# A gated recurrence on one core: the four loads of wx issued from two queues in turn, the biases after them

## The chip, the cores and the metric

The kernel runs on one core of a Trainium2 chip. The metric is the time of one execution on the device in microseconds (us); of several runs the median is taken. The profile comes from one further execution.

## What is computed

Eight sequences (B = 8) of 512 steps with 512 features go through a recurrent cell with a state of 512, and its output is added to the input. All is fp32.

```python
def step(h, x_t):
    fused = sigmoid(concatenate([x_t, h], axis=-1) @ w_W + w_b)
    hidden_state, output_state = split(fused, 2, axis=-1)
    memory_state = x_t @ wx_W + wx_b + hidden_state * (h @ wh_W + wh_b)
    h_new = output_state * h + (1.0 - output_state) * tanh(memory_state)
    return h_new, h_new

_, hs = scan(step, h0, swapaxes(x, 0, 1))    # 512 steps, h0 = cond_1024
return x + swapaxes(hs, 0, 1)
```

The 512 steps depend on each other; only the products of x with its weights can be made ahead.

## The kernel before

The 512 features lie as 4 quarters (k) of 128 partitions. The weights are held in SBUF in three tiles, each cut by k:

- `wx`: the weights that multiply x, four parts of 768 KB (128 rows of 6 KB each), loaded at L118 to L120;
- `wgr`: the weights of the state for the banks R and G, four parts of 512 KB (L122 to L124);
- `whh`: those for bank H, one load of 768 KB for three parts and one of 256 KB for the fourth (L125 to L127).

Three smaller things are loaded too. `head` (L92, L93; 144 KB) holds x of the first eight steps and the initial state. `rows4` (L114 to L116; 8 KB) is set to zero, and the four rows of biases go into four of its partitions. x itself comes in chunks of 16 steps: `load_x` (L96) loads the second half of chunk 0 at L132, chunks 1 to 3 after the first three steps (L374), and later ones as buffers come free.

A load is issued by an engine's queue. Here SyncE's queue issues everything but `head` and the biases, which ScalarE's queue issues before ScalarE's first arithmetic, the loading of its function table and a sigmoid of one column (L158). A load signals through one of eight completion counters, handed out in the order of the program; the ninth load takes the first counter again and its issue waits until the load that had it has landed.

The work that precedes the recurrence stands in the kernel in this order, and each engine does its part of it in this order:

1. TensorE starts its banks with zeros (L184) and multiplies zeros twice (L189, `warm` at L190), each as two records of 512 columns.
2. The bias matmul (L191) spreads `rows4` over the partitions by a matrix `ones`, into the PSUM bank `xp0`. It needs the biases landed.
3. VectorE copies that bank to the tile `bias` (L193) and the initial state into its tiles (L196). ScalarE's `seed` (L213) copies `bias` into the other bank, `xp1`.
4. `prefill(0)` (L215) adds, into `xp0`, the products of x of the first four steps with `wx`: for each k four matmuls of 384 columns side by side, two records each, so 8 records for a quarter and 32 in all. The quarter k needs part k of `wx`. It begins after VectorE's copy, since it adds to what the copy reads.
5. One more `warm`; ScalarE's `spread` (L230) copies `xp0` into the banks R, G and H; VectorE's `turn_x` (L235) transposes a part of it.
6. Step 0 (FIRST, L29): TensorE does the state's products for R and G, quarter by quarter ("Q0" to "Q3", from `wgr`), with the four quarters of `prefill(1)` between them ("x"), and then bank H (from `whh`). From step 1 on the order is that of L27, with one quarter of the next group's prefill behind it.

In every step VectorE transposes the banks and ScalarE takes sigmoids and a tanh of them; VectorE's scan (L283) makes the new state, in two halves, `hTA` and `hTB`, and TensorE's next matmuls on bank R need `hTA`. Of matmuls all records stand at L178 (the helper `mm`), so they are told apart by their tiles.

The loads touched by the change are these, with the helper for x between them and `head`:

```python
nc.scalar.dma_start(out=head, in_=xh)                     # L93
...
nc.vector.memset(rows4, 0.0)                              # L115
nc.scalar.dma_start(out=rows4[0:128:32], in_=bias_d)      # L116
...
for k in range(NQ):
    nc.sync.dma_start(out=wx[:, k], in_=wx_d[k])          # L120
```

Of the kernel before, what the change touches and what calls it, by code (L numbers as in the profile page):

```python
# [36 lines left out]
def tile_cond_rnn_residual(  # L37
# [39 lines left out]
    nc = tc.nc  # L77
# [35 lines left out]

    rows4 = const.tile([P, 512], F32, name="rows4")  # L114
    nc.vector.memset(rows4, 0.0)  # L115
    nc.scalar.dma_start(out=rows4[0:128:32], in_=bias_d)  # L116

    wx = const.tile([P, NQ, NQ, 384], F32, name="wx")  # L118
    for k in range(NQ):
        nc.sync.dma_start(out=wx[:, k], in_=wx_d[k])  # L120

    wgr = const.tile([P, NQ, NQ, 256], F32, name="wgr")  # L122
    for k in range(NQ):
# [134 lines left out]
    for i in range(T):  # L258
# [8 lines left out]
        for n in (ORDER if i else FIRST).split():  # L267
# [3 lines left out]
            bank, k = n[0], int(n[1])  # L271
# [210 lines left out]
```

## Time and profile before

| | |
|---|---|
| median of 3 runs | 1693.86 us (1693.85 to 1693.97) |
| the profiled execution | 1693.49 us |
| its span, first to last instruction | 1691.7 us |
| granted TensorE clock over the span | 1.000 |
| PE busy | 1680.3 us, 99% of the span |
| DVE, ACT, POOL busy | 64%, 54%, 14% of the span |
| DMA | 30.86 MB in all; mean 18 GB/s over the span |
| DMA in 3 to 7 us, 7 to 11, 11 to 15, 15 to 18 | 410, 423, 420, 411 GB/s |
| SyncE's issues of wx | 4 from 0.74 us, 0.38 to 1.05 us each |
| wx, issue to landing | 5.1 to 9.3 us, median 7.2 |
| ScalarE's issue of head | 0.74 us, lasting 0.42; 5.2 to landing |
| ScalarE's issue of the biases | 1.43 us, lasting 1.09 |

PE is TensorE's matmul, PEld its loading of weights, DVE VectorE, ACT ScalarE, POOL GpSimd, SP SyncE; SPq and ACTq are the queues by which an engine issues loads. A row of the timeline has the start, the length, the engine, the line of the kernel, the operation, the tile written and the tiles read, the shape and the number of instructions merged; in brackets stands how long the engine had been idle before, and what ended that by the profile. Releasers are inferred from the events of semaphores, so where several things were awaited the name can be wrong. Matmuls overlap, so a record is longer than the time from one start to the next. In a table by stages the columns are the stage, its length, busy time and count of instructions of PE, PEld, DVE, ACT and POOL, the granted clock, the share of the 16 DMA engines that was busy, and GB/s.

### The profile page before, as it was taken

The page shows a single profiled execution, that of the slowest core. Times are in us where ns is not written, and L with a number is a line of the kernel's source. Part 1 is how long each engine was busy: PE and PEld are TensorE (multiplying, and loading weights), DVE is VectorE, ACT ScalarE, POOL GpSimd, SP SyncE. Part 2 cuts the span into 40 slices and gives each one's busy share as a digit, 9 for nine tenths or more (in the row PEclk, how much of TensorE's full clock was granted, in tenths as well). Part 3 has the DMA queues.
Part 4 walks back from the last instruction along what each step waited for, and adds up shares of the span by engine and source line. Part 5 has one row for each costly group of instructions (what it writes and reads, how often), then busy time and mean ns, then how long its engine had stood idle before and what let it go on. Part 6 is the DMA issues. An engine that isn't in the chain of part 4 may idle for free.

```text
span 1691.7 us, 121258 instructions
## 1 busy us (share of the span) xinstructions
PE 1680.3 (99%) x53230; PEld 1467.6 (87%) x53230; DVE 1087.0 (64%) x8229; ACT 915.5 (54%) x5121; POOL 231.2 (14%) x1032
## 2 busy tenths in 40 slices
PE   8999999999999999999999999999999999999998
PEld 6888888888888888888888888888888888888887
DVE  5666666666666666666666666666666666666666
ACT  3555555555555555555555555555555555555554
POOL 0111111111111111111111111111111111111111
PEclk9999999999999999999999999999999999999999
DMA  4000000000000000000000000000000000000000
GB/s 177 17 17 5 17 17 17 17 4 17 17 17 17 4 17 17 17 17 13 9 18 17 17 17 4 17 17 17 17 5 17 17 17 17 4 17 11 11 11 10
DMA packets 11483, 30.86 MB, mean 18 GB/s; under 512 B 1220, under 2 KB 1732, under 8 KB 10952
## 3 DMA queue, kind: packets, MB, share of 16 engines
q1 hardware_dynamic: 10800, 22.94, 3.9%
q8 instruction: 416, 6.82, 1.7%
q14 instruction: 115, 0.94, 0.2%
q10 hardware_dynamic: 152, 0.16, 0.0%
HBM read 14.70 MB, written 8.39 MB: 14 GB/s over the span
## 4 chain that ended last, share of the span: by engine, by line
PE 98%; DMA 1%; DVE 0%; ACT 0%; issue 0%; SPq 0%
PE R L178 26%; PE G L178 26%; PE H L178 26%; PE xp L178 19%; DMA whh<-in_whh_dram 1%; DMA head<-in_xh_dram 0%; DVE md1A L321 0%; DVE hTA L283 0%; ACT hd0A L205 0%; ACT hTA L205 0%; SPq L124 0%; DVE tz L303 0%; ACT hTB L205 0%; DVE hTB L283 0%; ACT hd0B L205 0%
## 5 line engine op out<-in xcount | busy, mean ns | idle before, releaser
L178 PE MATMUL xp<-wx,xin 128*32 128x384 f32 x4032 | 431.3, 486 | 0.0
L178 PEld LDWEIGHTS R<-wgr,hTA 128*32 128x32 f32 x8176 | 247.4, 135 | 206.8 <-DVE hTA L283 206.4
L303 DVE STREAM_TRANSPOSE tr<-R 128x64 f32<-128x64 f32 x1022 | 194.4, 229 | 309.1 <-PE R L178 309.1
L178 PE MATMUL R<-wgr,hTA 128*32 128x128 f32 x8176 | 330.9, 273 | 2.2 <-DVE hTA L283 2.2
L178 PE MATMUL H<-whh,hTA 128*32 128x128 f32 x8192 | 331.3, 273 | 0.8 <-DMA whh<-in_whh_dram 0.8
L178 PE MATMUL H<-whh,hTB 128*32 128x128 f32 x8192 | 331.2, 273 | 0.0
L178 PE MATMUL R<-wgr,hTB 128*32 128x128 f32 x8176 | 330.6, 273 | 0.0
L178 PE MATMUL G<-wgr,hTB 128*32 128x128 f32 x8176 | 330.6, 273 | 0.0
L178 PE MATMUL G<-wgr,hTA 128*32 128x128 f32 x8176 | 330.6, 273 | 0.0
L385 POOL TENSOR_TENSOR ot<-xin,hTB 128x16 f32<-128x16 f32 x503 | 126.4, 251 | 1415.6 <-DVE hTB L283 1324.0
L205 ACT ACTIVATE hd0B<-tz 128x16 f32<-128x16 f32 x512 | 114.9, 224 | 305.3 <-DVE tz L303 305.3
L205 ACT ACTIVATE md0A<-tr 128x16 f32<-128x16 f32 x512 | 119.6, 234 | 265.2 <-DVE tr L303 265.2
L178 PEld LDWEIGHTS H<-whh,hTA 128*32 128x32 f32 x8192 | 260.2, 136 | 1.2 <-DMA whh<-in_whh_dram 1.2
L178 PEld LDWEIGHTS G<-wgr,hTA 128*32 128x32 f32 x8176 | 259.8, 136 | 0.0
L178 PEld LDWEIGHTS H<-whh,hTB 128*32 128x32 f32 x8192 | 254.5, 122 | 0.0
L178 PEld LDWEIGHTS G<-wgr,hTB 128*32 128x32 f32 x8176 | 254.1, 122 | 0.0
L178 PEld LDWEIGHTS R<-wgr,hTB 128*32 128x32 f32 x8176 | 245.2, 122 | 0.0
L283 DVE TENSOR_TENSOR_SCAN hTA<-hd0A,hTA 128x48 f32<-128x48 f32 x512 | 132.1, 258 | 149.2 <-ACT hTA L205 149.2
L283 DVE TENSOR_TENSOR_SCAN hTB<-hd0B,hTB 128x24 f32<-128x24 f32 x1024 | 158.1, 196 | 104.0 <-ACT hTB L205 104.0
L205 ACT ACTIVATE hd0A<-tz 128x16 f32<-128x16 f32 x512 | 118.9, 232 | 111.4 <-DVE tz L303 111.4
L321 DVE STREAM_TRANSPOSE md1A<-G 128x64 f32<-128x64 f32 x511 | 156.8, 307 | 28.7
L205 ACT ACTIVATE hTB<-hTB 128x16 f32<-128x16 f32 x512 | 121.2, 237 | 81.1 <-DVE hTB L283 80.5
(62 smaller groups left out, 1680.2 us busy)
## 6 DMA issues: line engine op xcount, KB each, us to landing
xin<-in_x_dram SPq DMA_DIRECT2D x31, 256.0 KB, 3.8
out_dram<-ot SPq DMA_DIRECT2D x31, 256.0 KB, 3.3
wx<-in_wx_dram SPq DMA_DIRECT2D x4, 768.0 KB, 7.2
wgr<-in_wgr_dram SPq DMA_DIRECT2D x4, 512.0 KB, 9.7
whh<-in_whh_dram SPq DMA_DIRECT2D x1, 768.0 KB
whh<-in_wh_dram SPq DMA_DIRECT2D x1, 256.0 KB, 11.2
out_dram<-ot SPq DMA_DIRECT2D x1, 192.0 KB, 1.9
head<-in_xh_dram ACTq DMA_DIRECT2D x1, 144.0 KB, 5.2
```

Of the source, the lines that this page charges most:

```text
L178: nc.tensor.matmul(out_, lhsT, rhs, start=start, stop=False, skip_group_check=True)
L205: inst = nc.scalar.activation(out_, in_, func, **kw).ins
L283: nc.vector.tensor_tensor_scan(*[t_[:, :, c_].rearrange("p n c s -> p (n c s)") for t_ in (out_, d0, d1)], 0.0, ALU.mult, ALU.add,)
L303: inst = nc.vector.transpose(t_.rearrange("p c n -> p (c n)"), raw[n][hf]).ins
L321: nc.vector.transpose(md1[hf][g % 2][:, :, :, 0].rearrange("p n c -> p c n"), raw["h"][hf])
L385: return engine.tensor_tensor(ot[:, t, 2 * hf : 2 * hf + 2, :].rearrange("p c n -> p n c"), x_of(c, slice(2 * hf, 2 * hf + 2), t, 1).rearr ...
```

## The change

The loads of parts 1 and 3 of `wx` are issued by ScalarE's queue, those of parts 0 and 2 by SyncE's as before, and the load of the biases is issued by ScalarE's queue after them. In the built program SyncE's queue begins with wx 0, wx 2 and the loads of `wgr`, and ScalarE's with head, wx 1, wx 3 and the biases, ahead of the function table; the completion counters follow the new order. The instructions of TensorE, VectorE and GpSimd and their order are the same.

```diff
     rows4 = const.tile([P, 512], F32, name="rows4")
     nc.vector.memset(rows4, 0.0)
-    nc.scalar.dma_start(out=rows4[0:128:32], in_=bias_d)
 
     wx = const.tile([P, NQ, NQ, 384], F32, name="wx")
     for k in range(NQ):
-        nc.sync.dma_start(out=wx[:, k], in_=wx_d[k])
+        (nc.scalar if k % 2 else nc.sync).dma_start(out=wx[:, k], in_=wx_d[k])
+    nc.scalar.dma_start(out=rows4[0:128:32], in_=bias_d)
```

## The prediction, made before the changed kernel ran

> **What bounds the kernel now.** I read the chain that ended last first. It is PE nearly all the way, so anything that delays the first step of the recurrence by some us, with nothing later that waits and could absorb it, is added to the end. The same chain in order of time shows where PE is not yet the bound: the first 18.2 us.
>
> ```profile
> PE 98%; DMA 1%; DVE 0%; ACT 0%; issue 0%; SPq 0%
> ```
> ```profile
> 0.74 5.23 DMA head<-in_xh_dram
> ...
> 6.83 11.38 DMA whh<-in_whh_dram
> 18.21 0.04 issue
> 18.25 1.11 PE H L178 x32
> 19.36 0.65 PE xp L178 x8
> 20.01 0.44 PE R L178 x16
> ```
>
> (Columns: start, length, what.) The last wait for data is whh. Then I read the timeline of the start-up, because the change moves two loads there, and one of them, the biases, opens everything.
>
> ```profile
> 6.77 1.10 PE L178 MATMUL xp<-rows,ones 128*128 128x512 f32 x2 [0.57 <-DVE hTB L160]
> ...
> 7.91 0.69 DVE L193 COPY bias<-xp 128x512 f32<-128x512 f32 x1 [1.26 <-PE xp L178]
> ...
> 8.65 2.14 PE L178 MATMUL xp<-wx,head 128*32 128x384 f32 x24 [0.78 <-DVE bias L193]
> ...
> 11.44 0.85 PE L178 MATMUL xp<-wx,head 128*32 128x384 f32 x8 [0.64 <-DMA wx<-in_wx_dram]
> ...
> 12.36 0.25 ACT L230 COPY R<-xp 128x128 f32<-128x128 f32 x1 [3.14 <-PE xp L178]
> ...
> 13.22 0.27 DVE L235 STREAM_TRANSPOSE md1B<-xp 128x32 f32<-128x32 f32 x2
> ...
> 13.59 0.67 PE L178 MATMUL xp<-wgr,hTA 128*32 128x256 f32 x8 [0.24 <-issue]
> ...
> 18.25 0.67 PE L178 MATMUL H<-whh,hTA 128*32 128x128 f32 x16 [0.77 <-DMA whh<-in_whh_dram]
> ...
> 18.82 0.26 DVE L283 TENSOR_TENSOR_SCAN hTA<-hd0A,hTA 128x48 f32<-128x48 f32 x1 [0.36 <-ACT hTA L205]
> ...
> 19.82 0.62 PE L178 MATMUL R<-wgr,hTA 128*32 128x128 f32 x16
> ```
>
> The reader is to see a serial chain: biases landed, bias matmul (L191), VectorE's copy (L193), prefill(0) from 8.65, its last quarter held to 11.44 by the fourth part of wx, then the spreads, the transposes of L235, and step 0 at 13.59. The releaser named at 6.77 is inferred. The built program lets that matmul wait for the biases' counter and for the memsets of ones, and the latter ended at 2.21 + 0.47 = 2.68; so the biases landed at about 6.7.
>
> Last, the DMA queues (q1 is SyncE's, q10 ScalarE's: packets, MB, share), in 3.5 to 4.5 us, and then the GB/s by stages.
>
> ```profile
> q1 hardware_dynamic: 59, 0.36, 86.3%
> q10 hardware_dynamic: 58, 0.07, 18.5%
> ```
> ```profile
> 7.00:11.00 4.00, 3.01 (x26) 0.72 (x25) 1.01 (x5) 0.59 (x1) 0.00 (x0) 1.00 1.01 423
> 11.00:15.00 4.00, 3.32 (x34) 1.49 (x38) 0.51 (x4) 0.59 (x3) 0.00 (x0) 1.00 1.03 420
> ```
>
> The engines are full (share 1.01 to 1.03, 420 GB/s), so a second queue cannot bring more bytes there. While both queues hold work they are served packet for packet, 59 to 58, though a packet of wx is 6 KB and one of head 1.2 KB.
>
> **The change, part by part.** *SyncE's queue* loses two issues of about 0.4 us. Its two loads of wgr come earlier on its ring, but the ring was already fed six loads ahead of the data, so this gains nothing. The eight completion counters are handed out in program order, so the later issues wait for: wgr 2 head, wgr 3 wx 0, whh wx 1, whh3 wx 2, then the x loads wx 3, wgr 0, the biases and wgr 1. wx 1 will land at about 9.6 instead of 7.6, so whh is issued some 3 us later, with 2.1 MB of wgr still in front of it (5 us at 420 GB/s): no hole, whh lands near 18.2 as before. The x loads that now wait longer are first read from step 8 on, beyond 40 us.
>
> *ScalarE's queue* gets two issues ahead of the biases, and behind them the table load and the sigmoid of L158. An issue took 0.42 to 1.10 us in the rows, so the last of these ends near 6 instead of 4.05; ScalarE's next work waits for the bias copy (8.63 before, later now). Cost nothing.
>
> *The biases* now stand behind head, wx 1 and wx 3 on ScalarE's ring, and that ring gets every second packet. A load of 128 rows puts 8 packets and one for its counter on each of 16 engines. The biases' row is ScalarE's packet 28 (3 x 9 + 1). SyncE's ring had 26 packets done over 16 engines (1.6 each) when ScalarE's first came at 2.75 us, so by then it has served about 30: wx 0, wx 2, wgr 0 (27) and three rows of wgr 1. In MB: ScalarE 0.147 + 2 x 0.786 + 0.008 = 1.73; SyncE 2 x 0.786 + 0.524 + 3/8 x 0.524 = 2.29; together 4.02. Before, wx 3 landed at 11.4 with 3.30 MB behind it (issued at 2.1, 9.3 to landing). So the biases land at 11.4 + (4.02 - 3.30) / 0.42 = 13.1. The same reckoning for the biases of before (1.24 MB) gives 6.5 against 6.7 seen, so I take 13.2: **6.5 us later**. Bounds: shared by bytes instead of packets (2 x 1.73 + the lead 0.16 = 3.62 MB) 12.2; all of wgr 1 ahead of them (4.35 MB) 13.9.
>
> A page puts the bounds otherwise: the Trainium skill ("DMA: Bandwidth & Descriptors", section "Queues, rings and completion order") says that an engine stays on a ring for a packet of typically 9 to 17 descriptors before it switches. By that a whole load would go at a turn, and the biases would come behind wgr 1, at 13.9. The rows' even count in each quarter us (15 to 15) speaks for single rows; I keep 13.2.
>
> *What absorbs some of it.* (1) The prefill's wait for wx 3. The four quarters of prefill(0) run at 0.65 each (0.325 for four matmuls in the rows from 8.65), so the last could have begun at 8.65 + 1.95 = 10.60 and began at 11.44: 0.84 of the delay goes there, since all of wx has landed by 12.9. (2) The wait for whh at 18.25. Without it, step 1's matmuls R could begin 0.77 earlier by PE, but they also need hTA, ready at 18.82 + 0.26 = 19.08, plus the 0.15 that the next step takes from there (22.94 to 23.09): 19.23 in place of 19.82, so 0.59. Sum: 6.5 - 0.84 - 0.59 = **5.07 us**. What is late next is only PE's chain itself, all of it shifted; each further step repeats at 3.27 us.
>
> *TensorE's clock.* PE has nothing between the end of the zero matmuls (6.21) and 13.2: 7 us. Before, its longest pause after the start was under 1 us. The rows show two speeds of the same 512-column fp32 matmul, while the granted clock reads 1.00 in both:
>
> ```profile
> L178 PE MATMUL xp<-zeros 128*128 128x512 f32 x4 | 3.5, 1036 | 0.0
> ```
> ```profile
> L178 PE MATMUL xp<-rows,ones x2: 592/630/667, 6.8 to 7.3; 128*128 128x512 f32 x2
> ```
>
> At 2.69, 3.64 and 4.49 one started each 0.85 us; at 6.77 the pair ran at 0.51. So a PE that had been idle ran slow from 2.07 to about 6.0 (the fourth, 857 ns against 1061, is part fast). No row has an idle of 7 us. Bounds: full speed, 0; or slow through bias matmul and prefill. Slow costs the matmul pair 1.91 in place of 1.10 and its weights 0.15, so 0.95; then prefill starts at 13.24 + 1.91 + 0.95 = 16.1, and at 0.85/0.51 its 2.6 us become 4.3 to 4.7: up to 2.1 more, 3.1 in all. I take the row of the cold start, which is nearer to 7 us of idleness than the pauses under 1 us: slow for 3.9 us from 13.24, to 17.1, so the first 1.0 us of prefill at 1/1.7 speed, 0.45. **1.4 us.** The spreads and transposes are not PE's and keep their times.
>
> The skill's page "TensorE: Matmul & The Clock Gate" (section "Part 1: The HAM clock gate") says that one idle window of about 3.4 us halves the clock and one busy window restores it, with windows that run free. By it the slow state is certain after 7 us and lasts 3.4 to 6.8 us: 1.2 to 2.9 us, varying from run to run.
>
> Together 5.07 + 1.4 = **6.5 us**. The profiled execution took 1693.49 (span 1691.7 and 1.8 around it), 0.37 under the median of the runs; set on the median, 1693.86 + 6.5 = **1700.4 us**.
>
> **Rivals.** (a) The clock holds: 5.1, so 1698.9. For it: granted clock 1.00 throughout. Against: two paces under that same 1.00. (b) Late and cold: biases at 13.9 and slow through prefill, 5.8 + 3.1 = 8.9, so 1702.8. For it: no row says when a second warm-up ends. (c) Not slower: ScalarE's ring is served ahead of SyncE's when both ask. Then the biases need only 1.73 + 0.16 MB, landing at 8.0; prefill starts at 9.9 and its third quarter waits for wx 2, last now, at 11.4; it ends 0.65 later, whh's 0.59 takes that back: 1693.9. It decides from biases at 8.1 down; with a warm clock the time stays within 0.2% (3.4 us, what a measurement here can tell from no change) up to 11.5. Against it: 59 to 58 packets, and head, a sixth of wx 0, landing with it (both near 5.9). (d) The loads get faster as a whole by two queues: only the 68 and 143 GB/s of 1 to 3 us leave room, and the biases' place stays: at best 1.5 us off the forecast, 1698.9.
>
> **How the numbers follow.** Forecast 0.60, (a) with (d) 0.22, (b) 0.13, (c) 0.05. Range 1697.9 to 1702.8: down to the warm clock with biases at 12.2 (4.1 us), up to (b). Slower by over 0.2%: 0.95; within 0.2%: 0.04; faster: 0.01.
>
> **What would show it.** After: the bias matmul near 13.2 (before 6.77), with its two records nearer 1000 than 600 ns; prefill's four quarters without a wait for wx; H without a wait for whh; q10 holding some 1.7 MB; step 0's first matmul at 20 to 21; steps 3.27 us as before. The forecast is wrong if the biases land before 11.5, or if whh lands late.

## The result and the profile after

The changed kernel takes 1701.33 us (median of 5 runs, 1700.68 to 1701.54), the kernel before 1693.97 us (1693.85 to 1694.11): ratio 1.0043, 95% interval 1.0032 to 1.0054, slower by 7.4 us. The profiled execution took 1700.68 (span 1698.9), the fastest of the five; against the profiled execution of before, 1693.49, it is 7.19 slower.

The chain that ended last, in order of time (start, length, what), begins differently now. Where head and whh stood, the load of the biases stands alone:

```profile
2.15 10.38 DMA rows<-in_bias_dram
12.53 0.14 issue
12.67 2.06 PE xp L178 x2
14.75 0.70 DVE bias L193
15.50 5.58 PE xp L178 x34
```

The timeline of the start-up, the lines that answer to those of before:

```profile
12.67 2.05 PE L178 MATMUL xp<-rows,ones 128*128 128x512 f32 x2 [6.69 <-DMA rows<-in_bias_dram]
...
14.75 0.69 DVE L193 COPY bias<-xp 128x512 f32<-128x512 f32 x1 [8.11 <-PE xp L178]
...
15.50 4.52 PE L178 MATMUL xp<-wx,head 128*32 128x384 f32 x32 [0.78 <-DVE bias L193]
...
21.34 0.67 PE L178 MATMUL xp<-wgr,hTA 128*32 128x256 f32 x8 [0.26 <-issue]
...
25.02 0.65 PE L178 MATMUL H<-whh,hTA 128*32 128x128 f32 x16
...
26.57 0.26 DVE L283 TENSOR_TENSOR_SCAN hTA<-hd0A,hTA 128x48 f32<-128x48 f32 x1 [0.36 <-ACT hTA L205]
...
26.88 0.67 PE L178 MATMUL R<-wgr,hTA 128*32 128x128 f32 x16
```

TensorE sat idle for 6.69 us; the biases had landed at 12.53. After that no matmul waits for wx or whh any more: the 32 of prefill(0) are one group, and H has no bracket. But the two bias matmuls take 2.05 us (1.10 before) and prefill's group 4.52. By stages (last three columns: granted clock, DMA share, GB/s):

```profile
8.00:9.00 1.00, 0.00 (x0) 0.00 (x0) 0.00 (x0) 0.00 (x0) 0.00 (x0) 0.91 1.01 414
9.00:19.00 10.00, 5.55 (x26) 1.69 (x30) 1.01 (x5) 0.59 (x1) 0.00 (x0) 0.50 1.02 416
19.00:20.00 1.00, 1.00 (x13) 0.17 (x5) 0.00 (x0) 0.00 (x0) 0.00 (x0) 0.97 1.05 406
```

The clock was granted at half from about 8.82 (0.18 of the first stage at 0.50 gives its mean of 0.91) to 19.06. The DMA columns are as before, full and at some 415 GB/s. The queues (packets, MB, share) in 6 to 11 us:

```profile
q10 hardware_dynamic: 207, 1.17, 56.4%
q1 hardware_dynamic: 206, 0.93, 44.9%
```

One packet of each queue in turn: in the first eight quarters of a us from 6 us on, the packets of q10 and q1 number 13 and 5, 5 and 12, 11 and 9, 10 and 7, 6 and 11, 12 and 5, 5 and 12, 11 and 5. ScalarE's rows of 6 KB carry more bytes than SyncE's, some of which are rows of wgr of 4 KB. Step 1 begins 7.06 us later (26.88 against 19.82) and lasts 3.37 us in place of 3.27; from step 2 on the steps are those of before, 7.16 later (30.25 against 23.09), and the span is 7.2 longer.

### The profile page after: what moved, and what is told of

The parts are those of the page before. It is cut to its first block, busy times and chain, and to the rows that moved or that the text cites. A ratio compares the mean times of both kernels' runs of the same rounds, so it can differ in the third digit from the quotient of the medians.

```text
span 1698.9 us, 121258 instructions
## 1 busy us (share of the span) xinstructions
PE 1682.6 (99%) x53230; PEld 1465.2 (86%) x53230; DVE 1088.5 (64%) x8229; ACT 916.4 (54%) x5121; POOL 231.8 (14%) x1032
## 3 DMA queue, kind: packets, MB, share of 16 engines
q8 instruction: 416, 6.82, 1.7%
## 4 chain that ended last, share of the span: by engine, by line
PE 98%; DMA 1%; DVE 0%; ACT 0%; issue 0%; DVEq 0%
PE R L178 26%; PE G L178 26%; PE H L178 26%; PE xp L178 20%; DMA rows<-in_bias_dram 1%; DVE md1A L321 0%; DVE hTA L283 0%; ACT hd0A L205 0%; ACT hTA L205 0%; DVE tz L303 0%; DVE bias L193 0%; DVE zeros L149 0%; DVE rows L115 0%; DVE tr L303 0%; ACT hTB L205 0%
```

## The experiments

The theory: the 6 us by which the biases come late, less what the waits for wx 3 and whh give back, make some 4.3 us, and the slow clock after TensorE's idle time makes the rest. The rivals put the loss on the split itself, on ScalarE's queue, or leave the clock out. The kernel before ran beside each group at 1693.77 and 1693.78 us.

**The biases' line moved alone.**

```diff
-        (nc.scalar if k % 2 else nc.sync).dma_start(out=wx[:, k], in_=wx_d[k])
+        nc.sync.dma_start(out=wx[:, k], in_=wx_d[k])
```

> All of wx stays on SyncE's queue; only the biases' line stands behind wx, still on ScalarE's queue, so that only head is ahead of them on their ring. Theory: nothing moves, biases near 6.7 us, 1694.0 us (within 0.3). Rival (the later line, or the other completion counter, costs by itself): more than 1 us over the kernel before.

Measured 1693.73 us (ratio 1.000, 0.999 to 1.0009); the bias matmul starts at 6.62:

```profile
6.62 1.43 PE L178 MATMUL xp<-rows,ones 128*128 128x512 f32 x2 [0.22 <-DMA rows<-in_bias_dram]
```

A later line costs nothing while only head is ahead on the ring. The pair's 1.43 us in place of 1.10 cost nothing either: the last quarter of prefill(0) waited for wx 3 as before (until 11.55).

**The split with the biases' line in its old place.** The changed kernel, with that line back ahead of wx.

> wx is split over the two queues, but the biases stay ahead of it on ScalarE's. Theory (the biases' place and the slow clock cost nearly all): biases land near 6.7 us as before, prefill(0) starts near 8.7, its last quarter waits for wx 3 until about 12.9 (landed then in the changed kernel) in place of 11.44, and some 0.7 of this 1.4 comes back at the wait for whh: +0.7 us, 1694.7 us. Rival (the split itself, wx arriving late, is what costs): near the changed kernel, above 1699 us.

Measured 1697.79 us (ratio 1.0024, 1.0014 to 1.0034), 4.0 over the kernel before: the expectation missed. The edit did not do what it was to do. The kernel's scheduler, not the order of the lines, places these issues, and it put wx 1 ahead of the biases, probably because these wait for the memset of their tile, which ends at 1.39 us. The timeline:

```profile
1.18 0.45 ACTq L120 DMA_DIRECT2D wx<-in_wx_dram  x1
...
1.67 1.08 ACTq L116 DMA_DIRECT2D rows<-in_bias_dram  x1
...
2.78 0.34 ACTq L120 DMA_DIRECT2D wx<-in_wx_dram  x1
...
9.58 2.05 PE L178 MATMUL xp<-rows,ones 128*128 128x512 f32 x2 [3.57 <-DMA rows<-in_bias_dram]
```

So this kernel shows the biases behind one part of wx in place of two: landed at 9.44, and the matmul pair slow again, after an idle time of only 3.57 us.

**The biases between wx 1 and wx 3, by the line's place.**

```diff
         (nc.scalar if k % 2 else nc.sync).dma_start(out=wx[:, k], in_=wx_d[k])
-    nc.scalar.dma_start(out=rows4[0:128:32], in_=bias_d)
+        if k == 1:
+            nc.scalar.dma_start(out=rows4[0:128:32], in_=bias_d)
```

> The changed kernel with the biases between wx 1 and wx 3 on ScalarE's ring: packet 19 of that ring in place of 28. Theory of packet for packet service: about 2.6 MB moved ahead of them, so they land at 9.3 to 9.8 us; prefill(0) then starts near 11.5 and waits for no wx after its second quarter: 1695.5 us if the clock stays up over an idle time of some 3.5 us, up to 1698.2 if it goes down. Rival (the landing doesn't follow the place in the ring): biases near 12.6, 1701 us, or near 6.7, 1694.7 us.

Measured 1698.25 us (ratio 1.0026, 1.0016 to 1.0037), bias matmul at 9.73: the same order on ScalarE's queue as in the experiment above, and the same result within the spread of these runs (1697.34 to 1698.40 there, 1697.63 to 1698.75 here). With 0, 1 and 2 parts of wx ahead of them the biases' matmul starts at 6.6 to 6.8, 9.6 to 9.7 and 12.7: 3 us for each part, in which the other queue's packets take their half. The time was at the upper end of what was expected: the clock did go down.

**The split with the biases really first.** The issue of the biases and of wx stands in a block of fixed order.

```diff
+    with tc.manual_schedule():
+        nc.scalar.dma_start(out=rows4[0:128:32], in_=bias_d)
+        for k in range(NQ):
+            (nc.scalar if k % 2 else nc.sync).dma_start(out=wx[:, k], in_=wx_d[k])
```

> wx split over the two queues, with the issue of the biases held ahead of wx 1 on ScalarE's queue by a fixed order of these loads (in the first try at this the scheduler had put wx 1 in front of the biases). Theory (the place of the biases costs, the split hardly): biases near 6.7 us, prefill(0) from about 8.7, its last quarter waits for wx 3 until about 13.0 in place of 11.44; of these 1.5 us some 0.7 come back at the wait for whh; TensorE's idle times stay under 3 us and the clock at 1.00: 1694.6 us. Rival (the split itself costs): above 1697 us.

Measured 1695.36 us (11 runs, 1694.91 to 1695.52; ratio 1.0009, 1.0000 to 1.0018). Timeline:

```profile
1.43 1.08 ACTq L118 DMA_DIRECT2D rows<-in_bias_dram  x1
...
2.55 0.89 ACTq L120 DMA_DIRECT2D wx<-in_wx_dram  x2
...
6.69 1.10 PE L178 MATMUL xp<-rows,ones 128*128 128x512 f32 x2 [0.66 <-DVE hTB L160]
...
13.78 0.85 PE L178 MATMUL xp<-wx,head 128*32 128x384 f32 x8 [1.64 <-DMA wx<-in_wx_dram]
```

The biases are on time, the bias matmul fast, and 5.8 of the 7.4 us are gone. The split keeps a price of 1.6 (the interval just touches 1, but the slowest run of the kernel before, 1694.01, is below the fastest here): wx 3 comes at 13.7, 0.7 later than expected. A likely reason, not tried by itself, is that the biases' issue now holds up wx 1's by more than 1 us (2.55 against 1.18 in the changed kernel). Step 0 begins at 15.94 against 13.59, 2.35 later, of which 0.69 comes back at whh. In the changed kernel wx 3 landed at 12.9 and this price was hidden behind the biases.

**No split, the biases last on SyncE's queue.**

```diff
-        (nc.scalar if k % 2 else nc.sync).dma_start(out=wx[:, k], in_=wx_d[k])
-    nc.scalar.dma_start(out=rows4[0:128:32], in_=bias_d)
+        nc.sync.dma_start(out=wx[:, k], in_=wx_d[k])
+    nc.sync.dma_start(out=rows4[0:128:32], in_=bias_d)
```

> No split: all of wx on SyncE's queue and the biases behind it on the same queue, so that one ring brings 3.3 MB before them and no wgr gets in between. Theory: biases near 11.3 us, TensorE idle from 6 to 11.3 us, clock down to 0.50; 4.6 later, less 0.84 and 0.69 regained at wx and whh, plus 1.2 to 2.9 for the clock: 1698.2 to 1699.9 us. Rival (the loss belongs to ScalarE's queue or to two queues at work): near 1694 us.

Measured 1699.45 us (ratio 1.0035, 1.0021 to 1.0048), in the expected range. With no second queue at work most of the loss is there, so it belongs to what stands ahead of the biases. Two lines of its timeline:

```profile
11.15 2.05 PE L178 MATMUL xp<-rows,ones 128*128 128x512 f32 x2 [4.74 <-DMA rows<-in_bias_dram]
11.59 2.78 SPq L101 DMA_DIRECT2D xin<-in_x_dram  x4
```

The second row is the issue of x, which waits for the completion counter of wx 3; so wx 3 landed just before 11.59, and the biases, behind it on the same ring, had landed at 11.01.

**The changed kernel with TensorE kept busy.**

```diff
     mm(xps[1], zeros[:, :128], zeros, start=True)
-    warm()
+    for _ in range(7):
+        warm()
```

> The changed kernel with six more pairs of zero matmuls ahead of the bias matmul, which fill TensorE's idle time from 6 to about 11 or 12 us; the biases land as late as in the changed kernel. Theory (2.7 us of the loss are slow TensorE clock after the idle time: 0.95 in the bias matmul, 1.74 in prefill): granted clock 1.00 from 6 us on, bias matmul records near 600 ns, 1701.3 - 2.7 = 1698.6 us. Rival (the clock costs nothing on the path, all of the loss is the late biases): 1701.3 us.

Measured 1698.05 us (9 runs, 1697.87 to 1698.12; ratio 1.0025, 1.0015 to 1.0035). Timeline:

```profile
12.62 1.10 PE L178 MATMUL xp<-rows,ones 128*128 128x512 f32 x2 [1.42 <-DMA rows<-in_bias_dram]
...
14.50 2.79 PE L178 MATMUL xp<-wx,head 128*32 128x384 f32 x32 [0.79 <-DVE bias L194]
...
18.59 0.67 PE L178 MATMUL xp<-wgr,hTA 128*32 128x256 f32 x8 [0.25 <-issue]
...
24.13 0.67 PE L178 MATMUL R<-wgr,hTA 128*32 128x128 f32 x16
```

The biases come at the same time (12.62 against 12.67), the pair takes 1.10 in place of 2.05 and prefill 2.79 in place of 4.52. Between the medians this is 3.3 us (3.1 if each is first set against the kernel before that ran beside it), between the profiled executions 2.8 (1700.68 and 1697.92). The spread of the runs falls from 0.86 to 0.25 us. So the clock's part is shown, and what is left, 4.3 us over the kernel before, is the late biases at full clock.

**No split, biases last on SyncE's queue, TensorE kept busy.** The same edit, with six in place of seven.

> As the kernel with no split and the biases last on SyncE's queue, with five more pairs of zero matmuls that fill TensorE's idle time to about 10.3 us. Theory (the late biases cost 3.1 us at full clock, the slow clock is the rest): clock 1.00 throughout, 1697.0 us, and runs that agree within 0.3 us, since no idle window is left for the clock. Rival (the clock costs nothing here): the same as without the zero matmuls.

Measured 1696.51 us (11 runs, 1696.40 to 1696.63; ratio 1.0016, 1.0007 to 1.0025). The zero matmuls lasted until the biases were there, and the pair and prefill were fast:

```profile
11.23 1.10 PE L178 MATMUL xp<-rows,ones 128*128 128x512 f32 x2
...
13.11 2.79 PE L178 MATMUL xp<-wx,head 128*32 128x384 f32 x32 [0.79 <-DVE bias L194]
```

Without them prefill's group took 4.73 us. The clock's part here is 2.9 us and that of the late biases 2.7; the time is 0.5 under the expected one.

**The kernel before with bank H later in step 0.**

```diff
-FIRST = "Q0 x Q1 x Q2 x Q3 H0 H1 H2 H3"
+FIRST = "Q0 x Q1 x Q2 x Q3 x H0 H1 H2 H3"
...
-        take(later, 1)
+        if i:
+            take(later, 1)
```

> The kernel before with one line of its order changed: in step 0 the fourth quarter of prefill(1) stands before bank H and not behind it. Theory (the wait for whh in step 0 is the only thing there that holds the chain, and it absorbs about 0.6 us of any delay): the quarter, 0.65 us, fills the wait of 0.77, H starts at 18.25 as before, and step 1 begins some 0.6 us earlier: 1693.2 us. Rival (the wait is cover for nothing, the chain is held by hTA): 1693.8 us.

Measured 1693.61 us against 1693.78 (ratio 0.9999, 0.9991 to 1.0008): 0.17 us, not separable from nothing, and less than expected. In its timeline the wait for whh has shrunk, but the second half of the state is now late:

```profile
18.47 0.67 PE L178 MATMUL H<-whh,hTA 128*32 128x128 f32 x16 [0.17 <-DMA whh<-in_whh_dram]
...
20.76 0.66 PE L178 MATMUL R<-wgr,hTB 128*32 128x128 f32 x16 [0.29 <-DVE hTB L284]
```

hTB needs bank H, which is no earlier here (18.47 against 18.25); in the changed kernel H came earlier relative to all the rest. So the 0.69 that the wait for whh gives back to a delay was not had by filling that wait. No version found is clearly faster than the kernel before.

## Why the prediction was right

The sign, the place and the order of the terms held; the time was 1701.33 where 1700.4 was forecast. Term by term, from the starts in the profiles of before, of after and of the kernel with TensorE kept busy:

| term | predicted, us | measured, us | from |
|---|---|---|---|
| biases later | +6.5 | +5.9 | bias matmul 6.77, then 12.67 |
| no wait for wx 3 | -0.84 | -0.85 | kept busy: prefill 5.85 later, step 0 5.00 later |
| less wait for whh | -0.59 | -0.69 | step 0 7.75 later, step 1 7.06 later |
| slow clock in the bias matmul | +0.95 | +0.95 | the pair 2.05 against 1.10 |
| slow clock in prefill | +0.45 | +1.75 | prefill to step 0: 5.84 against 4.09 kept busy |
| sum | 6.5 | 7.06 | 7.19 between the profiled executions |

Two sizes were off, by 0.6 and 1.3 us, and partly cancelled; that the total came within 0.9 us is in part luck. The third, smaller difference is a shift in time: step 1 began 0.05 after hTA was ready, not 0.15, and then lasted 0.10 longer, so that at step 2 (7.16 later) the wait for whh had given back the 0.59 reckoned.

*The landing of the biases*, predicted for 13.2, was 12.5. The packets were served one for one as reckoned (207 to 206), wx 3 landed at 12.9 as reckoned (the x load that waits for it was issued at 12.90), but the line of landings was laid through loads on 128 partitions, each of which ends with 16 packets of 4 bytes for its counter and has landed with the last of them; the biases are four rows with four such packets. The packet records of the trace show the difference: the biases' rows ended between 11.89 and 12.05 us, the last row of wx 3 at 12.40, and of the twenty counter packets of the two loads eighteen came by 12.21 and the last two, wx 3's, at 12.54 and 12.55. The kernel with the biases last on SyncE's queue shows the same: the biases' rows ended by 10.56 and landed at 11.0, the last two counter packets of wx 3 came at 11.20 and 11.24. So the biases lay on engines that were not the slowest. The estimate that the prediction made from the Trainium skill ("DMA: Bandwidth & Descriptors", "Queues, rings and completion order": typically 9 to 17 descriptors from one ring before an engine switches), a whole load at a turn and the biases at 13.9, does not fit: 207 to 206 packets in 5 us, both queues at work in every quarter of a us shown, and the biases at 12.5.

*The slow clock in prefill* was the step that failed in size. "Slow for 3.9 us from 13.24" was taken from the cold start; measured, it stayed at 0.50 for 6.4 us after the first matmul (12.67 to 19.06), through nearly all of prefill, near the upper bound that was given for this term (2.1). The rule of the Trainium skill's "TensorE: Matmul & The Clock Gate" ("Part 1: The HAM clock gate": free-running windows of about 3.4 us, a busy one of which is needed to speed up) was the better guide: the 1.2 to 2.9 us that the prediction estimated from it for the whole clock term holds the 2.7. This trace agrees with the windows: slow from 8.82 to 19.06 is 10.24 us, three times 3.41. Two slips of the working are small: the first two zero matmuls start 0.95 us apart, not 0.85, and 1.0 us at 1/1.7 speed costs 0.41, not 0.45.

Of the rivals, the clock that holds is what the kernel kept busy was made into: 4.3 over the kernel before where 5.1 was reckoned, the difference being the landing. "Late and cold" had its cold half come true. ScalarE's ring served first is excluded by the packets and the landing. Loads faster by two queues are excluded too: in 1 to 2 and 2 to 3 us the DMA engines moved 43 and 171 GB/s against 68 and 143 before, and from 3 to 18 us, in four stages, 412 to 418 against 410 to 423. The issues that the prediction set at nothing were so: whh was issued at 9.82, 3 us later than before, and still landed at 18.3 and its fourth part at 19.0, before H wanted them at 25.02; the table load ended at 4.59, far ahead of ScalarE's next need at 15.48.

## What to carry to other kernels

A small load that opens the work must stand at the head of its queue: where the DMA engines are already full, a second queue brings no bytes sooner, and every large load put ahead of the small one costs it more than its own transfer, because the other queue's packets go in between (3 us for each 768 KB, which alone are 1.9 us at 415 GB/s). When such a load is late, look also at what TensorE does meanwhile: an idle time of 3.4 us was enough to halve its clock for more than 6 us of the work that followed, and a few dummy matmuls in the gap gave back some 3 us. And read the built order of the issues, for a scheduler may undo a move of one line.

## What the runs showed of the hardware that was not expected

- TensorE's clock stayed at half for a whole number of equal windows. From the means of the stages it lasted 10.24 us in the changed kernel and 6.82 (8.90 to 15.72) with the biases behind one part of wx, by the place of their line ahead of wx:

```profile
8.00:9.00 1.00, 0.00 (x0) 0.00 (x0) 0.00 (x0) 0.00 (x0) 0.00 (x0) 0.95 1.00 412
9.00:15.00 6.00, 4.64 (x22) 1.32 (x26) 1.01 (x5) 0.59 (x1) 0.00 (x0) 0.50 1.02 420
15.00:16.00 1.00, 1.00 (x14) 0.35 (x9) 0.00 (x0) 0.00 (x0) 0.00 (x0) 0.64 1.06 438
```

  The other kernel of that order gives 6.82 too (9.64 to 16.46). These are three and two times 3.41, and the clock records of the traces say the same (10.24 and 6.83 us). In the changed kernel the window that would run from 12.23 to 15.65 had TensorE at work for about 2.2 of 3.41 us and did not bring the clock back; nor did about 2.5 of 3.41 us (9.63 to 13.05) with the biases' line between wx 1 and wx 3.
- The runs spread by 0.8 to 1.1 us where TensorE had idled for 3.4 us or more, and by 0.15 to 0.25 in the kernel with only the biases' line moved and in the two kept busy. A phase of the windows that differs from run to run would do this. The profiles do show a phase that differs: in nine of the ten the first clock record, at 1.00, begins between 5.40 and 7.31 us, and the later it begins the longer the zero matmuls ahead of it took: four of them 3.29 us in the changed kernel (5.40), 3.52 in the kernel before (5.87), 3.73 with only the biases' line moved (7.31), where the pair took 1.43 as well. That this makes the spread is not shown, and the split with the biases first, whose pair took the fast 1.10, spreads by 0.6 for a reason that stays open.
- The granted clock does not always show the half clock. With the biases last on SyncE's queue it read 1.00 in every stage, while the pair took the 2.05 us of the slow clock; and it reads 1.00 in the slow first microseconds too. In both cases that 1.00 is no reading: the trace holds no clock record there. The first record of that kernel begins at 17.95 us, so whether its TensorE came up to full clock before and went down again, or stayed slow from the start, is open. A recorded change from 1.00 to 0.50 after a pause stands in three profiles: the changed kernel and the two with the biases behind one part of wx. The duration of a known matmul is the safer sign.
- A load of four rows landed before a load of 128 rows that stood ahead of it on the same ring (11.0 against 11.5; 12.5 against 12.9 in the changed kernel).
